# Two-layer attention and perception kernel: spread key loads, five split half groups, shared value buffers, late pointwise weights

## The chip, the cores and the metric

The kernel runs on one core of a Trainium2 chip. The metric is the device time of one launch in microseconds; lower is better. Engines are named as in the profile: PE (matmul), PEld (weight load), DVE (VectorE), ACT (ScalarE), POOL (GpSimd) and SP (SyncE, which here only issues transfers).

## The reference

Input `x` is (4, 64, 64, 256) in float32. Two layers follow each other.

```python
# layer 0: full self-attention over the 4096 pixels of an image
q, k, v = x @ Wq + bq, x @ Wk + bk, x @ Wv + bv      # widths 32, 32, 256
attn = softmax(einsum('bnd,bmd->bnm', q, k))
h = gamma * (attn @ v) + x
# layer 1: depthwise 3x3 (3 outputs a channel), two pointwise layers, 3x3 local attention
perceived = depthwise_conv3x3(h, w_perc) + b_perc    # 256 -> 768 channels
hid = gelu(w_up1 @ perceived + b_up1)                # 768 -> 512
h_new = h + w_up2 @ hid + b_up2                      # 512 -> 256
out = h_new + local_attention3x3(h_new)              # softmax over 9 neighbours
```

## The kernel before

**Slots and points.** The 4 images are cut into 8 blocks of 512 pixels each, so there are 32 *slots* (`NSLOT`), one per block of queries, eight to an image. A slot runs over the image's 8 key blocks (*groups*, `G`), each in two halves of 256 keys, so it has 16 *points*. One software pipeline, written out by hand in the loop over slots and points, interleaves both layers. In each point the program emits, in this order: loads of keys and values for two groups ahead (`load_keys`, `load_values`), the energies and exponentials two points ahead (`energy`), the load of value forms three points ahead (`load_forms`), the jobs of layer 1 for older slots (`jobs[point]`), the weighted sum `product` of this point, the denominators of the next point (`add_up`), and a number of depthwise steps taken from `share[point]`. Each engine takes its instructions in this order. The depthwise conv (`perceive`) of a slot has 60 DVE steps: three rounds of 16 tap steps (L585) and 4 mixing steps (L591).

**Parts.** Most half groups are a plain fp32 product: 8 matmul instructions of `p` with `v` (L398). The half groups in `IN_PARTS` are done in parts: `p` and `v` are split into a high part, a remainder and a "gap" form, and 12 fp32r matmuls replace the 8 (L410). This costs ACT one more pass (`ph`, L384) and DVE two more (`pl` L429, `pg` L430), emitted in `add_up` one point before the product. The value forms are made once in `project_v` and kept in DRAM (`packed_f`). Slots 0 and 31 have no parts.

**End of a slot.** `partial_sums` turns the denominators (DVE, L453 and L454), a small matmul `dps` (PE, L472) adds them over partitions, and `finish` scales the four accumulator banks into the ring `xp`; the next slot's energies and jobs come behind `dps` on PE. The job `local_values` in point 10 leaves a PSUM bank that DVE must empty (`lv`, L887).

**Boundaries.** In slots 7, 15 and 23 the projections of the next image are done as well, after every second point (`nxt`): `project_v` twice and, for even blocks, `project_qk`, whose result `st` goes to DRAM (`packed`). Slot 0 does the same for the rest of the first image. Keys come back from `packed` with each row needed twice: `load_parts` uses two transfers of 64 rows, the outer dimension of the transfer being the 2.

**Buffers.** One ring of four buffers `late` holds `ph`, `pl`, `pg` and the loaded forms `vf`; `vs` (three) holds what `project_v` writes out; `st` is its own. Two buffers hold keys (`ka`), three hold values (`v`). PSUM has two `m` banks for all jobs and `dps`, four `acc` banks and one two-bank tile for energies.

Of the kernel before, what the change touches and what calls it, by code (L numbers as in the profile page):

```python
# [16 lines left out]
P = 128  # L17
# [33 lines left out]
BELOW = 1.0 - 2.0**-13  # L51
IN_PARTS = (2, 6, 10, 14)

# [5 lines left out]
def attention_then_perception_kernel(  # L59
# [37 lines left out]
    def unshifted():  # L97
# [113 lines left out]
        packed_f = tc.dram_tile([P, NSLOT * 2, 3, 2 * C], F32, name="packed_f")  # L211

        def in_parts(s, G, half):
            return 0 < s < NSLOT - 1 and 2 * G + half in IN_PARTS
# [37 lines left out]
        def project_qk(s):  # L252

            ps = bank("m", f"qk_{s}")
            for kin in range(CH):
                for r in range(2):
                    nc.tensor.matmul(
                        ps[2 * r * CQK : 2 * (r + 1) * CQK, :],
                        lhsT=wqk[:, kin].rearrange("p s d -> p (s d)"),
                        rhs=staged[s + r][:, kin, :], start=(kin == 0), stop=(kin == CH - 1),  # L260
                    )
            if s == 2:
                both = tile_of([P, TPB, C], "late", "st_2", 4).rearrange(
                    "p (a t) c -> p a (t c)", a=2
                )
            else:
                both = tile_of([P, 2, NB], "st", f"st_{s}")
            high, low = both[:, 0, :], both[:, 1, :]
            nc.scalar.activation(high.bitcast(F32R), ps, AF.Identity, bias=bqk2)
            nc.scalar.activation(low, ps, AF.Identity, bias=bqk2)  # L270
            nc.vector.tensor_tensor(low, low, high, ALU.subtract)
            if s == 0:
                queries[0] = tile_of([P, NB], "qa", "qa_0", 2)
                for G in range(2):
                    keys[0, G] = tile_of([P, NB], "ka", f"ka_0_{G}", 2)
                for part, G in ((0, 0), (1, 0), (0, 1), (1, 1)):
                    for i in range(2):
                        for to, at, from_ in (
                            (queries[0], 2 * i + part, 0), (keys[0, G], 2 * part + i, 2 * G + 1)
                        )[G:]:  # L280
                            rows, of = (slice(j * CQK, (j + 1) * CQK) for j in (at, from_))
                            nc.sync.dma_start(out=to[rows, :], in_=both[of, part, :])
            nc.sync.dma_start(
                out=packed[s // 2].rearrange("a r q d n -> (r q d) a n"), in_=both
            )

# [21 lines left out]
        def load_forms(s, G, half):  # L308
            forms[s, G, half] = tile_of([P, TPB, C], "late", f"vf_{s}_{G}_{half}", 4)
            nc.sync.dma_start(  # L310
                out=forms[s, G, half].rearrange("p (f t) c -> p f (t c)", f=2),
                in_=packed_f[:, 2 * block(s, G) + half, 1:3],
            )

        def fresh(name):
            return tile_of([P, 2, C], "vs", name, 3)

        def project_v(s, pair, tag="m"):
# [11 lines left out]
            if not split or s < NBLK or s >= NSLOT - NBLK:  # L330
                if s >= NBLK:
                    v = fresh(f"vs_{s}_{pair}")
                else:
                    if pair == 0:
                        values[0, s] = tile_of([P, TPB, C], "v", f"v_0_{s}", 3)
                    v = values[0, s][:, 2 * pair : 2 * pair + 2, :]
                nc.scalar.activation(v, of, AF.Identity, scale=SPLIT / (SPLIT + 1.0))
                nc.scalar.dma_start(
                    out=packed_v[:, bass.ts(2 * s + pair, 2 * C)],
                    in_=v.rearrange("p t c -> p (t c)"),  # L340
                )
            if split:
                whole, high, low = (fresh(f"v{n}_{s}_{pair}") for n in "whl")
                nc.scalar.copy(whole, of)
                nc.scalar.activation(high.bitcast(F32R), of, AF.Identity, scale=BELOW)
                nc.vector.tensor_tensor(low, whole, high, ALU.subtract)
                gap = fresh(f"vg_{s}_{pair}")
# [23 lines left out]
        def energy(s, G, half):  # L371
# [9 lines left out]
            weights[s, G, half] = p  # L381
            if in_parts(s, G, half):
                high = tile_of([P, 2, NB], "late", f"ph_{s}_{G}_{half}", 4)
                nc.scalar.activation(high.bitcast(F32R), p, AF.Identity, scale=BELOW)  # L384
                highs[s, G, half] = high

        def product(s, G, half):
            p = weights[s, G, half]
            first = G == 0 and half == 0
            if first:  # L390
                n = 2 * CH if 0 < s < NSLOT - 1 else CH
                accs[s] = [bank("acc", f"acc_{s}_{c}") for c in range(n)]
# [24 lines left out]
        def add_up(s, G, half):  # L417
# [8 lines left out]
            if in_parts(s, G, half):  # L426
                high = highs[s, G, half]
                low, gap = (tile_of([P, 2, NB], "late", f"p{n}_{s}_{G}_{half}", 4) for n in "lg")
                nc.vector.tensor_tensor(low.bitcast(F32R), p, high, ALU.subtract)  # L429
                nc.vector.scalar_tensor_tensor(  # L430
                    gap.bitcast(F32R), low, -SPLIT, high, ALU.mult, ALU.add
                )
                lows[s, G, half], gaps[s, G, half] = low, gap
# [32 lines left out]
        def finish(s, parts=((0, RB),)):  # L466
# [16 lines left out]
            for r0, r1 in parts:  # L483
                n = slice(r0 * W, r1 * W)
                for c, o in enumerate(os):
                    total = acc[c]
                    if 0 < s < NSLOT - 1:
                        nc.vector.tensor_tensor(o, acc[c], o, ALU.add)
                        total = o
                    nc.vector.scalar_tensor_tensor(  # L490
                        o[:, n], total[:, n], gam[:, 0:1], rden[:, n], ALU.mult, ALU.mult,
                        accum_out=seen(),
# [51 lines left out]
        def spare(s, name):  # L544
            tag = "v" if s == NSLOT - 1 else "late"
            return tile_of([P, TPB, C], tag, name, 3 if tag == "v" else 4).rearrange(
                "p (a t) c -> p a (t c)", a=2
            )

# [72 lines left out]

        wmix = pool.tile([P, 4, MULT, C], F32, tag="wmix", name="wmix")

        def mix_weights(y11, y12, y21, y22, t1, t2, t3, t4):
            for to, a, b in ((t1, y12, y11), (t2, y22, t1), (t3, y22, y12), (t4, y21, t2)):
                nc.gpsimd.tensor_tensor(to, a, b, ALU.subtract)
# [8 lines left out]
        def hidden_part(s, d, part):  # L638
# [8 lines left out]
            y22 = lambda j: wup1[:, MULT + j, bass.ts(d + 2, P)]  # L647
            t1, t2, t3, t4 = (lambda j, i=i: wmix[:, i, j, bass.ts(d, P)] for i in range(4))

# [343 lines left out]
        def local_reciprocal(s):  # L993
            inverse = tile_of([P, 2, NJ], "inverse", f"linverse_{s}")[:, 0, :]
            turned = tile_of([P, NB], "st", f"lturned_{s}")
            nc.vector.transpose(turned, totals.pop(s))
# [62 lines left out]
        nc.vector.tensor_scalar(gbv, gbv, gam[:, 0:1], None, ALU.mult)  # L1059
        nc.vector.tensor_scalar(gam, gam, 1.0 + 1.0 / SPLIT, None, ALU.mult)  # L1060
        wlv = pool.tile([P, CH, C], F32, tag="wlv", name="wlv")
# [10 lines left out]
        for slot in range(NSLOT):  # L1072
# [27 lines left out]

            share = [4, 4, 5, 6, 5, 3, 6, 4, 4, 4, 4, 4, 3, 2, 2, 0]
            if slot == NSLOT - 1:
# [21 lines left out]
            for point in range(points):  # L1124
                G, half = divmod(point, 2)
                after = slot + (G + 1) // NG, (G + 1) % NG
                if half == 0:
# [12 lines left out]
                for do in jobs[point]:  # L1140
                    do()
                product(slot, G, half)

# [17 lines left out]
                if slot == 0 and point == NG:  # L1161
# [8 lines left out]
                    mix_weights(  # L1170
                        *blocks_of(wup1, MULT, C), *(wmix[:, i] for i in range(4))
                    )
# [478 lines left out]
```

## Time and profile before

| | |
|---|---|
| median of 3 runs | 3391.0 us (3388.3 to 3391.58) |
| the profiled execution | 3390.54 us, of which the span of the program is 3388.7 us |
| PE busy | 3329.8 us (98% of the span) |
| DVE busy | 2833.7 us (84%) |
| ACT, POOL busy | 1256.2 us (37%), 413.1 us (12%) |
| mean granted TensorE clock | 0.993 |
| data moved by DMA | 358.51 MB, 106 GB/s over the span |

A row of a windows view gives a stretch of the span, then for each engine its busy time and number of instructions, then the granted clock (1.00 is full), the share of the 16 DMA engines' time in use and the rate. A timeline row gives start, length, engine, line, operation, tile written and tiles read, and how many instructions are merged in it; in brackets stands the idle time of the engine before it and who ended it. Instructions of one engine overlap a little in these rows, so costs below are taken from one start to the next.

### The profile page before, as it was taken

To read this page: it belongs to the slowest core of one execution; us is meant where nothing else is said; L and a number is where in the kernel's file an instruction comes from. 1 tells how busy PE (TensorE), PEld (TensorE's weight loads), DVE (VectorE), ACT (ScalarE), POOL (GpSimd) and SP (SyncE) were. 2 spreads that over 40 slices of the span, in tenths; PEclk is the share of its full clock that TensorE was granted. 3 is DMA by queue.
4 is the path that set the end of the run, shared out by engine and by line. 5 is a ranking of instruction groups with operands and counts; after the bars stand their busy time and mean duration, and the time that the engine had idled before them with its cause. 6 is when DMAs were issued, how large, how long until landed. Compare 5 with 4: busy or idle time off the path is not lost.

```text
span 3388.7 us, 33590 instructions
## 1 busy us (share of the span) xinstructions
PE 3329.8 (98%) x11654; PEld 2115.8 (62%) x11654; DVE 2833.7 (84%) x4188; ACT 1256.2 (37%) x1548; POOL 413.1 (12%) x590
## 2 busy tenths in 40 slices
PE   9989999999999999999999999999899999999998
PEld 5546666666666666666666666666566666666655
DVE  2488898877889998986898899887588999999995
ACT  3333434333433333333333433333333343333331
POOL 2100011101111100111011111101100111111031
PEclk9989999999999999999999999999999999999999
DMA  5432232353233323345333333324522333332100
GB/s 175 158 112 96 93 103 97 112 168 120 96 105 101 110 86 104 99 126 171 102 98 100 99 102 103 104 94 141 166 86 98 98 98 102 104 108 90 63 16 27
DMA packets 203109, 358.51 MB, mean 106 GB/s; under 512 B 71748, under 2 KB 72404, under 8 KB 202804
## 3 DMA queue, kind: packets, MB, share of 16 engines
q1 hardware_dynamic: 189972, 326.16, 30.6%
q0 software_dynamic: 4416, 15.11, 1.3%
q10 hardware_dynamic: 8544, 15.01, 1.2%
q8 instruction: 95, 1.56, 0.2%
q14 instruction: 82, 0.67, 0.1%
HBM read 303.01 MB, written 52.43 MB: 105 GB/s over the span
## 4 chain that ended last, share of the span: by engine, by line
PE 88%; issue 4%; DMA 3%; DVE 3%; ACT 1%; SPq 1%; POOL 0%; ACTq 0%; DVEq 0%; POOLq 0%
PE acc L398 37%; PE acc L410 9%; PE e L375 7%; PE dx L711 6%; PE hid_gf L654 4%; PE hid_de L654 4%; PE hid_bc L654 4%; PE lv L874 3%; PE g L807 3%; PE lo L1008 3%; PE s L915 2%; PE hid_a L654 2%; PE v L323 2%; DMA ka<-packed 2%; DVE perc L585 1%
## 5 line engine op out<-in xcount | busy, mean ns | idle before, releaser
L398 PE MATMUL acc<-p,v 128*128 128x512 f32 x3136 | 1421.2, 596 | 0.0
L585 DVE SCALAR_TENSOR_TENSOR perc<-xp,wperc,perc 128x526 f32<-128x526 f32 (+3 forms) x1554 | 1115.8, 778 | 31.1 <-ACT perc L581 31.0
L380 ACT ACTIVATE p<-e 128x1024 f32<-128x1024 f32 x512 | 523.9, 1023 | 1395.6 <-PE e L375 1215.7
L398 PEld LDWEIGHTS acc<-p,v 128*128 128x128 f32 x3136 | 593.8, 191 | 624.8 <-issue 610.9
L425 DVE TENSOR_TENSOR den<-den,p 128x1024 f32<-128x1024 f32 x480 | 593.5, 1236 | 45.4 <-ACT p L380 43.3
L375 PE MATMUL e<-qa,ka 128*128 128x512 f32 x1024 | 457.5, 528 | 30.2 <-DMA ka<-packed 17.3
L940 POOL TENSOR_TENSOR lp<-lp,near 128x396 f32<-128x396 f32 x60 | 86.6, 1443 | 2160.8 <-ACT lp L935 2160.8
L375 PEld LDWEIGHTS e<-qa,ka 128*128 128x128 f32 x1024 | 190.1, 190 | 214.6 <-issue 178.7
L711 PE MATMUL dx<-hid,wup 128*128 128x512 f32 x512 | 229.8, 592 | 0.0
L963 POOL TENSOR_TENSOR lsum<-lsum,lp 128x99 f32<-128x99 f32 (+1 forms) x179 | 176.0, 990 | 11.7
L654 PE MATMUL hid_de<-perc,wmix 128*128 128x256 f32 x720 | 165.0, 378 | 0.0
L591 DVE TENSOR_TENSOR perc<-perc 128x262 f32<-128x262 f32 x360 | 156.7, 449 | 6.3
L677 ACT ACTIVATE hid<-hid,bup 128x512 f32<-128x512 f32 x120 | 80.1, 715 | 216.5 <-DVE hid L661 216.5
L430 DVE SCALAR_TENSOR_TENSOR pg<-pl,ph 128x1024 fp32r<-128x1024 f32 x120 | 154.9, 1291 | 4.1
L711 PEld LDWEIGHTS dx<-hid,wup 128*128 128x128 f32 x512 | 96.9, 189 | 98.0 <-issue 92.8
L410 PE MATMUL acc<-ph,v 128*128 128x512 f32 x480 | 155.3, 445 | 0.0
L429 DVE TENSOR_TENSOR pl<-p,ph 128x1024 fp32r<-128x1024 f32 x120 | 150.5, 1254 | 0.0
L654 PEld LDWEIGHTS hid_de<-perc,wmix 128*128 128x128 f32 x720 | 135.9, 189 | 21.0
L581 ACT ACTIVATE perc<-xp,bperc,wperc 128x526 f32<-128x526 f32 (+1 forms) x192 | 147.2, 815 | 1.7 <-DVE xp L496 1.7
L410 PE MATMUL acc<-pl,vf 128*128 128x512 f32 x480 | 130.3, 393 | 4.4 <-DVE pl L429 4.4
L410 PE MATMUL acc<-pg,vf 128*128 128x512 f32 x480 | 129.6, 392 | 0.1
L384 ACT ACTIVATE ph<-p 128x1024 fp32r<-128x1024 f32 x120 | 127.0, 1058 | 3.8
(183 smaller groups left out, 3583.2 us busy)
## 6 DMA issues: line engine op xcount, KB each, us to landing
v<-packed_v SPq DMA_DIRECT2D x128, 512.0 KB
ka<-packed SPq DMA_DIRECT2D x508, 128.0 KB
vf<-packed_f SPq DMA_DIRECT2D x120, 512.0 KB
v<-packed_f SPq DMA_DIRECT2D x120, 256.0 KB
v<-packed_v SPq DMA_DIRECT2D x120, 256.0 KB
xp<-in_x SPq DMA_DIRECT2D x30, 528.0 KB
xc<-in_x SPq DMA_DIRECT2D x56, 256.0 KB
out<-lo SPq DMA_DIRECT2D x56, 256.0 KB
```

Of the source, the lines that this page charges most:

```text
L375: nc.tensor.matmul(e[:, i, :], lhsT=keys[s, G][:, bass.ts(2 * half + i, P)].bitcast(F32R), rhs=queries[s].bitcast(F32R), start=True, stop= ...
L380: nc.scalar.activation(p, e, AF.Exp)
L398: nc.tensor.matmul(accs[s][c], lhsT=v[:, i, bass.ts(c, P)], rhs=p[:, i, :], start=(first and i == 0), stop=(last and i == 1),)
L410: nc.tensor.matmul(accs[s][to + c], lhsT=w[:, i, bass.ts(c, P)].bitcast(F32R), rhs=x[:, i, :].bitcast(F32R), start=(to > 0 and n == 0 and ...
L425: nc.vector.tensor_tensor(den, den, p, ALU.add)
L429: nc.vector.tensor_tensor(low.bitcast(F32R), p, high, ALU.subtract)
L430: nc.vector.scalar_tensor_tensor(gap.bitcast(F32R), low, -SPLIT, high, ALU.mult, ALU.add)
L585: nc.vector.scalar_tensor_tensor(acc, win, wt, acc, ALU.mult, ALU.add)
L591: nc.vector.tensor_tensor(t[:, to, :], t[:, a, :], t[:, b, :], op)
L654: nc.tensor.matmul(ps[:, n * C : (n + 1) * C], lhsT=w(j), rhs=rows_of(mixes[s, j][:, kind, :]), start=(j == 0), stop=(j == MULT - 1),)
L711: nc.tensor.matmul(ps, lhsT=wup2[:, d, bass.ts(c, P)], rhs=hids[s][:, d, :], start=(d == 0), stop=(d == NHC - 1),)
L963: nc.gpsimd.tensor_tensor(to, to, near_ws[block, half][:, t_, of, :], ALU.add)
```

## The change

- `load_parts` issues four transfers of 32 rows where it issued two of 64, for keys and queries.
- `IN_PARTS` is (2, 5, 8, 11, 14) where it was (2, 6, 10, 14), so five half groups a slot are in parts; slot 2 (`LAG_PERC`) joins slots 0 and 31 in having none.
- The four `late` buffers go. `ph`, `pl`, `pg` have one buffer each, `vf` two. `ph` is made one point later, ahead of that point's exponential (`high_part`).
- `vs` has four buffers and also takes `st` (as two tiles, stored by two transfers) and a transposed tile; in the first image `st` uses `o`, in slot 2's pair `pg`. The copy `whole` of a split is dropped (`low` takes it), and the plain pair of a block is projected before the split pair.
- `w_up1` and `w_up2` are loaded in slot 1 where they were loaded in slot 0; one of the four mixed weight blocks is kept in place of a block of `wup1`, which is loaded again in the last slot.
- `share` is a new list, with the same sum of 60. The scaled gamma gets its own tile.

```diff
-IN_PARTS = (2, 6, 10, 14)
+IN_PARTS = (2, 5, 8, 11, 14)
+        def in_two_sums(s):
+            return 0 < s < NSLOT - 1 and s != LAG_PERC
         def load_parts(to, s, which):
             pair, r = divmod(s, 2)
-            part = packed[pair, :, r, which]
-            for i in range(2):
-                of = part[i : i + 1].to_broadcast([2, CQK, NB]) if which else part
-                nc.sync.dma_start(out=to[2 * i * CQK : 2 * (i + 1) * CQK, :], in_=of)
+            for i in range(4):
+                of = packed[pair, i // 2 if which else i % 2, r, which]
+                nc.sync.dma_start(out=to[i * CQK : (i + 1) * CQK, :], in_=of)
...
-                both = tile_of([P, 2, NB], "st", f"st_{s}")
-            high, low = both[:, 0, :], both[:, 1, :]
+                tag, bufs = ("o", 2) if s < NBLK else ("vs", 4)
+                parts = high, low = [tile_of([P, NB], tag, f"st_{s}_{i}", bufs) for i in range(2)]
...
-            nc.sync.dma_start(
-                out=packed[s // 2].rearrange("a r q d n -> (r q d) a n"), in_=both
-            )
+            for i, part in enumerate(parts):
+                nc.sync.dma_start(
+                    out=packed[s // 2, i].rearrange("r q d n -> (r q d) n"), in_=part
+                )
...
-            forms[s, G, half] = tile_of([P, TPB, C], "late", f"vf_{s}_{G}_{half}", 4)
+            forms[s, G, half] = tile_of([P, TPB, C], "vf", f"vf_{s}_{G}_{half}", 2)
...
-                whole, high, low = (fresh(f"v{n}_{s}_{pair}") for n in "whl")
-                nc.scalar.copy(whole, of)
+                low, high = (fresh(f"v{n}_{s}_{pair}") for n in "lh")
+                nc.scalar.copy(low, of)
...
-            return [lambda: project_v(s, 0), lambda: project_v(s, 1)] + pair
+            order = sorted(range(2), key=lambda n: 2 * (s % NBLK) + n in IN_PARTS)
+            return [lambda n=n: project_v(s, n) for n in order] + pair
...
+        def high_part(s, G, half):
+            high = tile_of([P, 2, NB], "ph", f"ph_{s}_{G}_{half}")
+            nc.scalar.activation(high.bitcast(F32R), weights[s, G, half], AF.Identity, scale=BELOW)
+            highs[s, G, half] = high
...
-        wmix = pool.tile([P, 4, MULT, C], F32, tag="wmix", name="wmix")
+        wmix = pool.tile([P, 3, MULT, C], F32, tag="wmix", name="wmix")
...
-            share = [4, 4, 5, 6, 5, 3, 6, 4, 4, 4, 4, 4, 3, 2, 2, 0]
+            share = [1, 3, 7, 7, 1, 3, 7, 3, 5, 6, 2, 5, 6, 1, 3, 0]
...
+                behind = slot + (point + 1) // points, *divmod((point + 1) % points, 2)
+                if in_parts(*behind):
+                    high_part(*behind)
                 if after[0] < NSLOT:
                     energy(*after, half)
...
+                if slot == NSLOT - 1 and point == NHC + 2 * RING:
+                    nc.sync.dma_start(out=wup1[:, :MULT, C:], in_=w_up1[:, :MULT, C:])
...
+                if slot == 1 and point == 2:
                     wup1 = loaded(w_up1, "wup1", queue=nc.gpsimd)
                     bup1 = loaded(b_up1, "bup1", queue=nc.gpsimd)
+                if slot == 1 and point == NG:
                     wup2 = loaded(w_up2, "wup2", queue=nc.gpsimd)
```

More of the change, by code (lines that the diff above doesn't have):

```diff
@@ L211, in unshifted @@
         packed_f = tc.dram_tile([P, NSLOT * 2, 3, 2 * C], F32, name="packed_f")
+        def in_two_sums(s):
+            return 0 < s < NSLOT - 1 and s != LAG_PERC
         def in_parts(s, G, half):
-            return 0 < s < NSLOT - 1 and 2 * G + half in IN_PARTS
+            return in_two_sums(s) and 2 * G + half in IN_PARTS
         def load_parts(to, s, which):
             pair, r = divmod(s, 2)
-            part = packed[pair, :, r, which]
-            for i in range(2):
-                of = part[i : i + 1].to_broadcast([2, CQK, NB]) if which else part
-                nc.sync.dma_start(out=to[2 * i * CQK : 2 * (i + 1) * CQK, :], in_=of)
+            for i in range(4):
+                of = packed[pair, i // 2 if which else i % 2, r, which]
+                nc.sync.dma_start(out=to[i * CQK : (i + 1) * CQK, :], in_=of)
         def fetch(s):
@@ L262, in project_qk @@
             if s == 2:
-                both = tile_of([P, TPB, C], "late", "st_2", 4).rearrange(
-                    "p (a t) c -> p a (t c)", a=2
-                )
-            else:
-                both = tile_of([P, 2, NB], "st", f"st_{s}")
-            high, low = both[:, 0, :], both[:, 1, :]
+                both = tile_of([P, 2, NB], "pg", "st_2")
+                parts = high, low = both[:, 0, :], both[:, 1, :]
+            else:
+                tag, bufs = ("o", 2) if s < NBLK else ("vs", 4)
+                parts = high, low = [tile_of([P, NB], tag, f"st_{s}_{i}", bufs) for i in range(2)]
             nc.scalar.activation(high.bitcast(F32R), ps, AF.Identity, bias=bqk2)
@@ L281, in project_qk @@
                             rows, of = (slice(j * CQK, (j + 1) * CQK) for j in (at, from_))
-                            nc.sync.dma_start(out=to[rows, :], in_=both[of, part, :])
-            nc.sync.dma_start(
-                out=packed[s // 2].rearrange("a r q d n -> (r q d) a n"), in_=both
-            )
+                            nc.sync.dma_start(out=to[rows, :], in_=parts[part][of, :])
+            for i, part in enumerate(parts):
+                nc.sync.dma_start(
+                    out=packed[s // 2, i].rearrange("r q d n -> (r q d) n"), in_=part
+                )
         def block(s, G):
@@ L315, in fresh @@
         def fresh(name):
-            return tile_of([P, 2, C], "vs", name, 3)
+            return tile_of([P, NB], "vs", name, 4).rearrange("p (t c) -> p t c", c=C)
         def project_v(s, pair, tag="m"):
@@ L333, in project_v @@
                 else:
-                    if pair == 0:
+                    if (0, s) not in values:
                         values[0, s] = tile_of([P, TPB, C], "v", f"v_0_{s}", 3)
@@ L342, in project_v @@
             if split:
-                whole, high, low = (fresh(f"v{n}_{s}_{pair}") for n in "whl")
-                nc.scalar.copy(whole, of)
+                low, high = (fresh(f"v{n}_{s}_{pair}") for n in "lh")
+                nc.scalar.copy(low, of)
                 nc.scalar.activation(high.bitcast(F32R), of, AF.Identity, scale=BELOW)
-                nc.vector.tensor_tensor(low, whole, high, ALU.subtract)
+                nc.vector.tensor_tensor(low, low, high, ALU.subtract)
                 gap = fresh(f"vg_{s}_{pair}")
@@ L381, in energy @@
             weights[s, G, half] = p
[L382 to L385, printed above, removed]
+        def high_part(s, G, half):
+            high = tile_of([P, 2, NB], "ph", f"ph_{s}_{G}_{half}")
+            nc.scalar.activation(high.bitcast(F32R), weights[s, G, half], AF.Identity, scale=BELOW)
+            highs[s, G, half] = high
         def product(s, G, half):
@@ L390, in product @@
             if first:
-                n = 2 * CH if 0 < s < NSLOT - 1 else CH
+                n = 2 * CH if in_two_sums(s) else CH
                 accs[s] = [bank("acc", f"acc_{s}_{c}") for c in range(n)]
@@ L427, in add_up @@
                 high = highs[s, G, half]
-                low, gap = (tile_of([P, 2, NB], "late", f"p{n}_{s}_{G}_{half}", 4) for n in "lg")
+                low, gap = (tile_of([P, 2, NB], f"p{n}", f"p{n}_{s}_{G}_{half}") for n in "lg")
                 nc.vector.tensor_tensor(low.bitcast(F32R), p, high, ALU.subtract)
@@ L486, in finish @@
                     total = acc[c]
-                    if 0 < s < NSLOT - 1:
+                    if in_two_sums(s):
                         nc.vector.tensor_tensor(o, acc[c], o, ALU.add)
@@ L490, in finish @@
                     nc.vector.scalar_tensor_tensor(
-                        o[:, n], total[:, n], gam[:, 0:1], rden[:, n], ALU.mult, ALU.mult,
+                        o[:, n], total[:, n], gam_parts[:, 0:1], rden[:, n], ALU.mult, ALU.mult,
                         accum_out=seen(),
@@ L544, in spare @@
         def spare(s, name):
[L545 to L548, printed above, removed]
+            if s == NSLOT - 1:
+                return tile_of([P, TPB, C], "v", name, 3).rearrange("p (a t) c -> p a (t c)", a=2)
+            spares.append(spares.pop(0))
+            return tile_of([P, 2, NB], spares[-1], name)
+        spares = ["ph", "pl", "pg"]
         def perceive(s, steps):
@@ L620, in unshifted, with mix_weights @@
         lower = by_turns(range(NPC), range(LOW, TAPS), RB - 1, RB)
-        wmix = pool.tile([P, 4, MULT, C], F32, tag="wmix", name="wmix")
-        def mix_weights(y11, y12, y21, y22, t1, t2, t3, t4):
-            for to, a, b in ((t1, y12, y11), (t2, y22, t1), (t3, y22, y12), (t4, y21, t2)):
+        wmix = pool.tile([P, 3, MULT, C], F32, tag="wmix", name="wmix")
+        def mix_weights(y11, y12, y21, y22, t1, t2, t4):
+            for to, a, b in ((t1, y12, y11), (t2, y22, t1), (t4, y21, t2), (y12, y22, y12)):
                 nc.gpsimd.tensor_tensor(to, a, b, ALU.subtract)
@@ L647, in hidden_part @@
             y22 = lambda j: wup1[:, MULT + j, bass.ts(d + 2, P)]
-            t1, t2, t3, t4 = (lambda j, i=i: wmix[:, i, j, bass.ts(d, P)] for i in range(4))
+            t1, t2, t4 = (lambda j, i=i: wmix[:, i, j, bass.ts(d, P)] for i in range(3))
+            t3 = lambda j: wup1[:, j, bass.ts(d + 2, P)]
             def products(name, *todo):
@@ L994, in local_reciprocal @@
             inverse = tile_of([P, 2, NJ], "inverse", f"linverse_{s}")[:, 0, :]
-            turned = tile_of([P, NB], "st", f"lturned_{s}")
+            turned = tile_of([P, NB], "vs", f"lturned_{s}", 4)
             nc.vector.transpose(turned, totals.pop(s))
@@ L1059, in unshifted @@
         nc.vector.tensor_scalar(gbv, gbv, gam[:, 0:1], None, ALU.mult)
-        nc.vector.tensor_scalar(gam, gam, 1.0 + 1.0 / SPLIT, None, ALU.mult)
+        gam_parts = pool.tile([P, 1], F32, tag="gam_parts", name="gam_parts")
+        nc.vector.tensor_scalar(gam_parts, gam, 1.0 + 1.0 / SPLIT, None, ALU.mult)
         wlv = pool.tile([P, CH, C], F32, tag="wlv", name="wlv")
@@ L1166, in unshifted @@
                     bperc = loaded(b_perc, "bperc", queue=nc.gpsimd)
+                if slot == 1 and point == 2:
                     wup1 = loaded(w_up1, "wup1", queue=nc.gpsimd)
                     bup1 = loaded(b_up1, "bup1", queue=nc.gpsimd)
+                if slot == 1 and point == NG:
                     wup2 = loaded(w_up2, "wup2", queue=nc.gpsimd)
                     mix_weights(
-                        *blocks_of(wup1, MULT, C), *(wmix[:, i] for i in range(4))
+                        *blocks_of(wup1, MULT, C), *(wmix[:, i] for i in range(3))
                     )
```

## The prediction

> **What bounds the kernel now.** I read the page's busy times first, then a windows view cut at the slots, then PE's waits, then the timelines of one steady slot.
>
> ```profile
> PE 3329.8 (98%) x11654; PEld 2115.8 (62%) x11654; DVE 2833.7 (84%) x4188; ACT 1256.2 (37%) x1548; POOL 413.1 (12%) x590
> ```
>
> ```profile
> 24.80:122.50 97.70, 89.83 (x267) 49.11 (x267) 28.94 (x35) 28.70 (x38) 18.51 (x24) 0.95 0.52 162
> 122.50:194.10 71.60, 66.78 (x208) 37.84 (x206) 38.45 (x44) 24.38 (x26) 0.62 (x2) 0.95 0.41 128
> 194.10:270.10 76.00, 69.35 (x201) 39.03 (x198) 72.82 (x105) 26.18 (x30) 0.61 (x2) 0.93 0.36 114
> 1817.20:1915.10 97.90, 97.90 (x345) 62.75 (x344) 88.98 (x133) 37.51 (x45) 11.85 (x14) 1.00 0.31 100
> 655.10:795.80 140.70, 135.06 (x505) 88.36 (x504) 97.85 (x145) 53.09 (x73) 15.04 (x26) 1.00 0.54 160
> 2306.40:2461.00 154.60, 141.56 (x505) 91.10 (x504) 97.85 (x145) 55.48 (x77) 15.68 (x26) 0.96 0.50 153
> ```
>
> Rows 1 to 3 are slots 0 to 2, row 4 the steady slot 18, the last two the boundary slots 7 and 23 (slot 15 has 140.9 us). A steady slot is PE without a gap; DVE is busy 89 of its 97.9 us. PE idles only at the start and at the boundaries, where the clock also falls below 1.00. So the gain must come from less PE work in steady slots, or from those gaps, and DVE has 9 us a slot to give.
>
> ```profile
> PE e L375 <- DMA ka<-packed: 17.3, 8, 4.8
> PE acc L410 <- DVE pl L429: 4.4, 2, 3.9
> ```
>
> Late keys are the longest of PE's waits. The end of the steady slot, on DVE from the `lv` of point 10 and on PE:
>
> ```profile
> 1884.36 0.76 DVE L887 TENSOR_TENSOR lv<-lv,blv 128x256 f32<-128x256 f32 x2 [1.47 <-PE lv L874]
> ...
> 1898.41 1.40 DVE L429 TENSOR_TENSOR pl<-p,ph 128x1024 fp32r<-128x1024 f32 x1
> 1899.85 1.48 DVE L430 SCALAR_TENSOR_TENSOR pg<-pl,ph 128x1024 fp32r<-128x1024 f32 x1
> ...
> 1907.59 0.69 DVE L454 TENSOR_REDUCE parts<-turned 128x16 f32<-128x512 f32 x1
> 1909.16 0.36 DVE L475 RECIPROCAL inverse<-dps 128x32 f32<-128x32 f32 x1 [0.88 <-PE dps L472]
> ```
>
> ```profile
> 1903.08 1.09 PE L410 MATMUL acc<-pl,vf 128*128 128x512 f32 x4
> ...
> 1908.82 0.30 PE L472 MATMUL dps<-parts,fold 128*128 128x32 f32 x2
> ```
>
> From 1884.36 to 1908.28 DVE never idles: 23.92 us. PE wants the sums at 1908.82, 0.54 us later. In the other steady slots this margin is 0.4 to 0.5 us (once less). DVE's spare time lies ahead of point 10; at the slot's end there is none. This is what decides.
>
> **Steady slots, PE.** In slot 1, where no jobs stand between:
>
> ```profile
> 179.26 3.60 PE L398 MATMUL acc<-p,v 128*128 128x512 f32 x8
> 182.30 1.03 PE L375 MATMUL e<-qa,ka 128*128 128x512 f32 x2
> 183.16 1.07 PE L410 MATMUL acc<-ph,v 128*128 128x512 f32 x4
> 184.07 1.07 PE L410 MATMUL acc<-pl,vf 128*128 128x512 f32 x4
> 184.98 1.07 PE L410 MATMUL acc<-pg,vf 128*128 128x512 f32 x4
> 185.88 0.62 PE L375 MATMUL e<-qa,ka 128*128 128x512 f32 x2
> ```
>
> A plain half group with the energies behind it takes 3.90 us (179.26 to 183.16), one in parts 3.18 (183.16 to the next plain product at 186.34): 0.7 us saved. 29 slots of 5 against 30 of 4 are 145 against 120: 25 x 0.7 = 17 us less PE work in all, 0.7 a steady slot.
>
> **Steady slots, DVE.** A further `pl` and `pg` cost 1.25 + 1.15 = 2.40 us from start to start where POOL is quiet. Over the slot they fit. Over its end they do not: before, points 10 to 15 hold one pair (for 14) and 15 steps of `share` (4+4+3+2+2+0); after, two pairs (for 11 and 14) and 17 steps (2+5+6+1+3+0). The steps come in rounds of 16 taps and 4 mixes; the four mixes of the third round lie in this stretch both times, so it gains two taps of 0.68. The stretch becomes 23.92 + 2.40 + 1.36 = 27.68 us. It starts 0.7 us sooner, since by point 10 three of five half groups are already in parts instead of two; the DVE idle ahead of `lv` (1.47 here, 1.97 in most slots) pays for the two steps more in points 7 to 9 and is then about 0.5. So the sums end 3.76 - 0.70 = 3.06 us later than now, PE has 0.45 us of margin, and the slot grows by 2.6 us to 100.5. PE shows it as two waits: about 1.7 us before `pl` at point 14 (`pl` would end near 1904.0 on this slot's clock; PE comes for it at 1903.08 - 0.70 = 1902.4) and the rest before `dps`. Where the slot's block has an edge row (6 of the 24), 0.8 us more border work in point 7 finds 0.5 us less idle: 0.35 each.
>
> That holds in slots 4 to 6, 8 to 14, 16 to 22 and 24 to 30: 24 x 2.6 + 6 x 0.35 = **+64 us**. Slot 3 has no local sums yet and stays.
>
> The uncertain part is POOL. Clean DVE work in the stretch adds up to 21.2 us; 2.7 us are delays while POOL multiplies masks and sums windows (L940, L963): a tap that meets L940 takes 1.38 instead of 0.68, `pl` and `pg` 0.2 more each, one `den` 0.5. After the change taps meet L963, which no steady slot shows. Bounds: 1.3 us less (only the L940 delays stay), +1.3 a slot, 31 us; 0.7 us more, +3.3, 80 us. I keep the sum of 2.7, since POOL's instructions are the same and DVE is never idle there in either.
>
> `ph` ahead of the exponential costs nothing: ACT idles 2 to 6 us ahead of most exponentials and `p` is a point old. Four key loads cost SP about 1 us more a group (0.5 an issue); a group lasts 10 us and more in a steady slot.
>
> **Start.** Adding up the points' excess over the same point without a gap, slot 0 loses 13.1 us, slot 1 8, slot 2 12.2, idle and half clock together. The key waits come from the transfer's shape: in the trace's semaphore records a key load issued at 236.05 us gets its last two engines' counts at 246.16, 10 us later, while a 32-row `ka<-st` issued at 11.43 has all sixteen by 13.40. The nearest row for the new loads is that one: 2 us, and 1 us more of issue. The Trainium skill ("DMA: Bandwidth & Descriptors", "Why a DMA increments its semaphore by 16 and not by 1") says that the number of engines divides the slowest dimension, so 2 for the old shape and 16 for the new; no run here shows it yet for a load from DRAM.
>
> Slot 0: late keys (7.4 us with the slow clock) leave about 2, since the first exponentials wait for `gbv`; the stop of ACT behind the weights' transfers (5.7 us) goes: -11. Slot 1: -8 of key stalls, -0.7, and +2 for the weights' 2 MB now beside its loads (0 if hidden, 6 if it stops SP as in slot 0, where one key issue took 7.6 us): -7. Slot 2: without parts 15 x 3.89 + 8.0 = 66.4 instead of 76.0, and DVE's 65 us fit: -9.5. Together **-27** (-16 to -33).
>
> **Boundaries.** 97.8 + 16 x 1.73 (`project_v`) + 4 x 1.87 (`project_qk`) = 133; the slots take 7, 7 and 21 us more. Spread keys remove the key waits and ACT's waits for stores queued on the two loaded engines. What is late next: `st` now shares `vs` with the forms. In block 4 ACT must wait with `st`'s low part until POOL's store of `low` has landed (DVE 1.8 us, issue 0.5, 2.7 to 4.4 to land), and queued behind it are `ph` and the exponential of points 11 and 12, and on DVE the subtraction of `st` with everything after: 2 us on PE, then some 2 at `dps`; and the split of block 7 now ends after the denominators, ahead of the reciprocal that frees an `m` bank: 1 to 1.5. I leave 5 us in each: -3, -3, -16 = **-22** (-12 to -37).
>
> **Sum.** 3390.5 + 64 - 27 - 22 = 3405.5; the profiled execution lies 0.5 us under the median, which I neglect.
>
> A rule against this change stands in "TensorE: Matmul & The Clock Gate" (The HAM clock gate): the clock halves after an idle window of 3.4 us. By it the new waits cost no clock. The trace is stricter: after 1.96 us idle up to 2423.33 the clock was 0.51 for 3.4 us, while 2.07 us up to 1612.18 cost none. Waits of 1.7 stay under both, so I add nothing.
>
> **Rivals.** (1) POOL's delays shrink because taps and POOL's short sums interleave better: below +2.05 us a slot (49 us over 24 slots) the change is a gain. For: nothing shows the new pairing. Against: a constant 2.7 us in 24 slots. At +1.3: 3390.5 + 33 - 49 = 3374. (2) The DVE end costs what I say, but start and boundaries give back all they lose (33 + 37): 3385. For: their causes are mostly DMA. Against: `st` behind the stores. (3) The loads do not spread, so the change doesn't do what it says: only slot 2 and ACT's stop gain some 15 us: 3440.
>
> **How the numbers follow.** Forecast 0.48, (1) 0.24, (2) 0.20, (3) 0.08. About 0.2% (7 us) is what a measurement of this kernel can tell from no change. Forecast and (3) give slower by more, except a sixth of the forecast: 0.48; (1) and half of (2) faster: 0.34; the rest 0.18. The forecast's own range is 3390 to 3436 (mainly 24 x 0.7 up, and 10 us of start and boundaries down). The whole range goes down to 3352, which is POOL's lower bound with the largest gains at start and boundaries (3390.5 + 31 - 33 - 37), and up to 3436.
>
> **What would show it.** Right: slots 0 to 2 near 87, 65 and 66 us; steady slots near 100.5 with PE waiting for `pl` and for `parts`; key waits gone. Wrong: steady slots at 97.2 without gaps, `lv` to sums under 25 us, or key loads whose last counts still come 10 us late.

## The result, and the profile after

The changed kernel takes 3414.8 us (median of 4 runs, 3413.4 to 3416.0) against 3389.7 us for the kernel before on the same chip: ratio 1.0074, 95% interval 1.0057 to 1.0092. It is slower by 25 us; 3405 was forecast. The profiled execution has a span of 3412.8 us, 24.1 us more than before.

The page's busy times and its row for the key loads (line, engine, operation, count, KB each, median us to landing):

```profile
PE 3330.4 (98%) x11754; PEld 2131.2 (62%) x11754; DVE 2901.1 (85%) x4248; ACT 1277.1 (37%) x1577; POOL 457.4 (13%) x602
ka<-packed SPq DMA_DIRECT2D x1016, 64.0 KB, 1.9
```

PE's busy time did not fall by the 17 us of work that five parts save, since part of each wait counts as busy: slot 21 takes 3.3 us more than the same five parts without waits (97.38 us, below), and the view has PE idle for 2.56 of them. Half clock counts as busy too, but the mean clock hardly moved (0.993 before, 0.994 after). The windows view by slots (columns as before; the rows are slots 0, 1, 2, then the steady slots 18 and 21, then the boundary slots 7 and 23):

```profile
25.00:110.90 85.90, 85.09 (x267) 47.27 (x266) 30.59 (x38) 29.60 (x40) 9.04 (x18) 1.00 0.56 166
110.90:179.40 68.50, 65.22 (x213) 38.57 (x211) 46.90 (x46) 24.46 (x26) 14.73 (x12) 0.98 0.54 170
179.40:245.80 66.40, 66.40 (x183) 33.98 (x182) 63.26 (x96) 21.65 (x24) 0.62 (x2) 1.00 0.38 108
1820.10:1921.40 101.30, 99.40 (x350) 64.31 (x349) 91.16 (x135) 38.16 (x46) 11.27 (x14) 0.98 0.33 102
2123.90:2224.60 100.70, 98.14 (x350) 63.25 (x349) 90.42 (x131) 38.20 (x46) 13.02 (x14) 1.00 0.33 102
642.20:777.30 135.10, 133.99 (x510) 89.20 (x509) 101.35 (x148) 54.56 (x75) 18.96 (x29) 1.00 0.59 176
2325.40:2461.50 136.10, 133.96 (x509) 89.05 (x508) 100.70 (x146) 57.56 (x80) 18.96 (x29) 1.00 0.61 184
```

Slot 0 lost 11.8 us, slot 1 3.1, slot 2 9.5, the three boundaries 5.6, 6.1 and 18.5. The steady slots grew: 100.7 us where there were 97.8. PE's waits (total us, times, longest) show on what:

```profile
PE acc L414 <- DVE pl L433: 39.6, 25, 2.0
PE dps L476 <- DVE parts L458: 14.9, 15, 1.1
PE e L378 <- ACT p L383: 5.4, 3, 3.2
```

The waits for keys (17.3 us before) are gone, and in their place stand the two that the prediction named. The timeline of the end of slot 21:

```profile
2190.49 0.75 DVE L894 TENSOR_TENSOR lv<-lv,blv 128x256 f32<-128x256 f32 x2 [0.32 <-PE lv L881]
...
2202.41 5.52 DVE L591 SCALAR_TENSOR_TENSOR perc<-xp,wperc,perc 128x526 f32<-128x526 f32 x6
2207.85 1.61 DVE L429 TENSOR_TENSOR den<-den,p 128x1024 f32<-128x1024 f32 x1
2209.38 1.39 DVE L433 TENSOR_TENSOR pl<-p,ph 128x1024 fp32r<-128x1024 f32 x1
2210.82 1.21 PE L414 MATMUL acc<-pl,vf 128*128 128x512 f32 x4 [1.49 <-DVE pl L433]
...
2217.45 0.69 DVE L458 TENSOR_REDUCE parts<-turned 128x16 f32<-128x512 f32 x1
2218.20 0.41 PE L476 MATMUL dps<-parts,fold 128*128 128x32 f32 x2 [0.94 <-DVE parts L458]
```

From `lv` to the end of the sums DVE takes 27.65 us without idling (27.68 was worked out). Six taps stand right ahead of the `den` and `pl` of point 14; PE waits 1.49 us for that `pl` and another 0.94 us for the sums, which come 0.06 us before PE starts `dps`.

Summed by groups of slots, from the first product of a slot to that of the next: the 24 steady slots +75.5 us, slot 3 +1.6, slots 0 to 2 -24.4, the boundaries -30.2, all together +22.5. Of the 1.6 us to the span's 24.1, 1.4 lie in the last 50 us of the program, where the profile's clock is 0.90 after and 0.94 before.

### The profile page after: what moved, and what is told of

It is laid out like the page before. It is cut to its first block, busy times and chain, and to the rows that moved or that the text cites. A ratio compares the mean times of both kernels' runs of the same rounds, so it can differ in the third digit from the quotient of the medians.

```text
span 3412.8 us, 34590 instructions
## 1 busy us (share of the span) xinstructions
PE 3330.4 (98%) x11754; PEld 2131.2 (62%) x11754; DVE 2901.1 (85%) x4248; ACT 1277.1 (37%) x1577; POOL 457.4 (13%) x602
## 4 chain that ended last, share of the span: by engine, by line
PE 74%; DVE 23%; issue 1%; ACT 1%; SPq 0%; DMA 0%; ACTq 0%; DVEq 0%; POOL 0%; POOLq 0%
PE acc L402 26%; DVE perc L591 10%; PE acc L414 8%; PE dx L718 6%; DVE den L429 5%; PE e L378 5%; PE hid_bc L661 5%; PE hid_gf L661 5%; PE hid_de L661 5%; PE v L325 3%; PE lv L881 3%; PE lo L1015 3%; PE g L814 2%; DVE pl L433 2%; PE hid_a L661 2%; DVE pg L434 2%
## 5 line engine op out<-in xcount | busy, mean ns | idle before, releaser
L402 PE MATMUL acc<-p,v 128*128 128x512 f32 x2936 | 1323.8, 594 | 0.2 <-ACT v L339 0.2
L402 PEld LDWEIGHTS acc<-p,v 128*128 128x128 f32 x2936 | 556.2, 191 | 586.7 <-issue 570.4
L414 PE MATMUL acc<-pl,vf 128*128 128x512 f32 x580 | 162.1, 402 | 39.6 <-DVE pl L433 39.6
L414 PE MATMUL acc<-ph,v 128*128 128x512 f32 x580 | 185.0, 441 | 0.0
L434 DVE SCALAR_TENSOR_TENSOR pg<-pl,ph 128x1024 fp32r<-128x1024 f32 x145 | 177.6, 1225 | 7.4
L433 DVE TENSOR_TENSOR pl<-p,ph 128x1024 fp32r<-128x1024 f32 x145 | 182.2, 1257 | 0.0
L414 PE MATMUL acc<-pg,vf 128*128 128x512 f32 x580 | 167.5, 412 | 3.1 <-DVE pg L434 0.3
L414 PEld LDWEIGHTS acc<-pl,vf 128*128 128x128 f32 x580 | 108.2, 190 | 74.0 <-DVE pl L433 51.2
L388 ACT ACTIVATE ph<-p 128x1024 fp32r<-128x1024 f32 x145 | 152.3, 1050 | 0.2
L414 PEld LDWEIGHTS acc<-pg,vf 128*128 128x128 f32 x580 | 110.3, 194 | 38.5 <-DVE pg L434 14.7
```

What stands on the lines that cost most here:

```text
L388: nc.scalar.activation(high.bitcast(F32R), weights[s, G, half], AF.Identity, scale=BELOW)
L402: nc.tensor.matmul(accs[s][c], lhsT=v[:, i, bass.ts(c, P)], rhs=p[:, i, :], start=(first and i == 0), stop=(last and i == 1),)
L414: nc.tensor.matmul(accs[s][to + c], lhsT=w[:, i, bass.ts(c, P)].bitcast(F32R), rhs=x[:, i, :].bitcast(F32R), start=(to > 0 and n == 0 and ...
L434: nc.vector.scalar_tensor_tensor(gap.bitcast(F32R), low, -SPLIT, high, ALU.mult, ALU.add)
```

## The experiments

All results in one table. Ratios are to the kernel before, run on the same chip. The last four columns are slot times in us from the profiled execution of each: the mean of the 24 steady slots, the sum of slots 0 to 2, slot 3, and the sum of the three boundary slots.

| kernel | median us | ratio, 95% | steady | 0 to 2 | 3 | 7+15+23 |
|---|---|---|---|---|---|---|
| before | 3389.7 | 1 | 97.70 | 245.2 | 94.8 | 436.2 |
| after | 3414.8 | 1.0074 (1.0057 to 1.0092) | 100.84 | 220.8 | 96.4 | 406.0 |
| after, old step list | 3376.4 | 0.9962 (0.9948 to 0.9976) | 99.32 | 218.6 | 94.3 | 406.9 |
| after, four parts, old list | 3338.9 | 0.9851 (0.9835 to 0.9868) | 97.89 | 217.4 | 94.9 | 407.5 |
| before, four key loads | 3366.4 | 0.9928 (0.9911 to 0.9944) | 97.69 | 223.9 | 94.8 | 436.3 |
| after, two key loads | 3451.7 | 1.0182 (1.0165 to 1.0199) | 100.83 | 238.5 | 96.4 | 425.3 |
| after, front-loaded list | 3329.9 | 0.9831 (0.9814 to 0.9847) | 97.38 | 220.7 | 94.3 | 407.3 |
| after, quiet POOL | 3345.7 | 0.9879 (0.9863 to 0.9896) | 98.12 | 220.9 | 94.9 | 405.9 |
| before, four key loads, new pair order | 3357.2 | 0.9913 (0.9896 to 0.9929) | 97.70 | 224.3 | 94.8 | 424.0 |
| after, early weights | 3409.6 | 1.0068 (1.0051 to 1.0085) | 100.88 | 216.7 | 96.4 | 406.0 |
| front-loaded list, early weights | 3325.8 | 0.9818 (0.9804 to 0.9831) | 97.35 | 215.9 | 94.3 | 407.2 |
| the same, six parts | 3307.9 | 0.9765 (0.9752 to 0.9779) | 96.76 | 215.9 | 94.4 | 403.6 |
| after, three `vs` buffers | 3423.2 | 1.0107 (1.0092 to 1.0123) | 100.87 | 219.3 | 96.4 | 415.3 |
| early weights, seven parts | 3369.7 | 0.9950 (0.9934 to 0.9967) | 98.91 | 220.8 | 95.4 | 406.7 |

### The end of the steady slot

**The old step list in the changed kernel.**

```diff
-            share = [1, 3, 7, 7, 1, 3, 7, 3, 5, 6, 2, 5, 6, 1, 3, 0]
+            share = [4, 4, 5, 6, 5, 3, 6, 4, 4, 4, 4, 4, 3, 2, 2, 0]
```

> The changed kernel with the step list of before (15 steps in points 10 to 15 where the new list has 17). Theory: DVE's stretch from lv to the sums sets the steady slot; two taps of 0.68 us less make it 27.7 - 1.36 = 26.3 us, so a steady slot falls from 100.7 to 99.3 us and the kernel from 3415 to about 3382 us (24 x 1.36 = 33 us). Rival A, POOL's delays set the length and the number of taps does not: steady slots stay at 100.7 us, 3415 us. Rival B, the new list is needed to fit five pairs into the middle of the slot: PE gets new waits before point 10 and the time is above 3415 us.

3376.4 us; the stretch from `lv` to the sums is 26.33 us in slot 21 and the slot 99.38. PE's long waits for `pl` are gone, the wait for the sums is left (two rows of the timeline, then PE's wait):

```profile
2162.78 0.75 DVE L894 TENSOR_TENSOR lv<-lv,blv 128x256 f32<-128x256 f32 x2 [1.67 <-PE lv L881]
...
2188.42 0.69 DVE L458 TENSOR_REDUCE parts<-turned 128x16 f32<-128x512 f32 x1
```

```profile
PE dps L476 <- DVE parts L458: 25.5, 22, 1.2
```

With the same five pairs, two taps moved ahead of `lv` are worth 38 us (1.53 us a steady slot, 1.36 expected), and the change is faster than the kernel before. Rivals A and B fall.

**Four parts.**

```diff
-IN_PARTS = (2, 5, 8, 11, 14)
+IN_PARTS = (2, 6, 10, 14)
```

with the old list again.

> The changed kernel with four half groups in parts (2, 6, 10, 14) and the step list of before; loads, buffers, order of the pairs and place of the weights stay as changed. Theory: the loss is all in the fifth pair and the steps at the slot's end, 24 x 3.15 = 75.6 us and 1.6 us in slot 3, less 0.7 us in slot 1: steady slots 97.8 us without gaps, 3415 - 76.5 = about 3338 us, below the kernel before by some 52 us. Rival: the single buffers of ph, pl and pg, or the exponential behind ph, cost something in steady slots by themselves: steady slots above 98.5 us, 3355 us or more.

3338.9 us, steady slots 97.89 us: within 1 us of the sum. So the fifth pair and the step list are the whole loss, and all the rest of the change (the buffers, `ph` a point later, the spread loads) costs a steady slot about 0.2 us.

**Without POOL's work at the slot's end.**

```diff
-                nc.gpsimd.tensor_tensor(pv, pv, mask, ALU.mult)
+                pass
...
-            nc.gpsimd.memset(t, 0.0)
-            for half in range(2):
-                for (block, t_), rows, of in pieces(s):
-                    to = tv[:, rows, columns(half)]
-                    nc.gpsimd.tensor_tensor(to, to, near_ws[block, half][:, t_, of, :], ALU.add)
+            nc.gpsimd.memset(t, 1.0)
```

> The changed kernel without POOL's multiplication by the neighbour mask and without its sums over windows (a constant stands in their place), so layer 1 leaves out the mask and its denominators. Theory: 2.7 us of DVE's 27.7 us from lv to the sums are delays beside POOL; without them the stretch is about 25 us, the steady slot 98.0 us, and the kernel 3415 - 24 x 2.7 = about 3350 us. Rival: the pairs and steps fill the 27.7 us by themselves and POOL costs little: stretch above 27 us, 3400 us or more.

3345.7 us; the stretch is 25.00 us and slot 21 takes 98.04 us (the windows view: POOL is busy 2.69 us of it, 13.0 in the changed kernel). The ends of the stretch in the timeline, then the slot in the windows view:

```profile
2147.88 0.76 DVE L894 TENSOR_TENSOR lv<-lv,blv 128x256 f32<-128x256 f32 x2 [0.32 <-PE lv L881]
...
2172.19 0.69 DVE L458 TENSOR_REDUCE parts<-turned 128x16 f32<-128x512 f32 x1
```

```profile
2081.30:2179.34 98.04, 97.59 (x349) 63.41 (x348) 87.73 (x131) 38.07 (x46) 2.69 (x8) 1.00 0.33 105
```

POOL delays DVE by 2.65 us in this stretch (27.65 - 25.00), as much as the 2.7 us that were worked out for the kernel before; the first rival of the prediction, that these delays shrink, is out.

**A list with less at the end.**

```diff
-            share = [1, 3, 7, 7, 1, 3, 7, 3, 5, 6, 2, 5, 6, 1, 3, 0]
+            share = [5, 4, 6, 6, 5, 4, 6, 4, 4, 4, 3, 3, 3, 1, 2, 0]
```

> The changed kernel with a third step list: 48 steps in points 0 to 9 and 12 in points 10 to 15 (the changed kernel has 43 and 17, the kernel before 45 and 15): [5, 4, 6, 6, 5, 4, 6, 4, 4, 4, 3, 3, 3, 1, 2, 0]. Theory: with three taps less at the end than with the list of before, the sums come 3 x 0.68 = 2.0 us sooner, less 0.4 us because lv then starts later; PE's last waits (1.2 us for the sums, 0.7 us at point 14) go, and the steady slot falls to 97.3 to 97.6 us, below the 98.0 us of four parts: 3376 - 24 x 2 = about 3328 us. Rival: the steps moved ahead delay the evictions of the hidden jobs, PE waits for a bank of m before point 10, and the steady slot stays at 98.5 us or more: 3352 us or more.

3329.9 us. Slot 21, in the windows view:

```profile
2069.28:2166.66 97.38, 97.38 (x350) 63.42 (x348) 90.37 (x131) 38.19 (x46) 12.89 (x14) 1.00 0.33 106
```

PE has no gap again and does five parts in 97.38 us; DVE is busy 90.37 us, just as in the changed kernel (90.42 of 100.7). Not DVE's amount of work cost 75 us but where in the slot it stands. `lv` did not come 0.4 us later, as I had it: DVE still idles 1.68 us ahead of it, as with the old list (1.67). The three steps moved forward fill DVE's other idle stretches ahead of it, which in slot 21 shrink from 5.7 to 3.8 us. The sums now come only 0.06 to 0.11 us before PE starts `dps`, so five parts with this list have no margin left at the slot's end.

### Start and boundaries

**Four key loads alone, in the kernel before.**

```diff
-            part = packed[pair, :, r, which]
-            for i in range(2):
-                of = part[i : i + 1].to_broadcast([2, CQK, NB]) if which else part
-                nc.sync.dma_start(out=to[2 * i * CQK : 2 * (i + 1) * CQK, :], in_=of)
+            for i in range(4):
+                of = packed[pair, i // 2 if which else i % 2, r, which]
+                nc.sync.dma_start(out=to[i * CQK : (i + 1) * CQK, :], in_=of)
```

> The kernel before with nothing changed but load_parts, which issues four transfers of 32 rows. Theory: the key waits (17.3 us) and the half clock and exponential waits that hang on them go: about -30 us, 3360 us, with slots 7, 15 and 23 near 137 us and steady slots at 97.8 us. Rival: the gain at start and boundaries came from the order of the pairs, st in two tiles and the late weights: -10 us or less, 3380 us or more.

3366.4 us: between the two. In the profiled execution all of the gain comes from slots 0 to 2 (-21.3 us) and the boundaries gain nothing; that execution is the slowest of four (3370.8 us), and where the two at 3363 us gain their 7 us was not seen. PE no longer waits for keys there, but one thing later. ACT in slot 7, from the timeline:

```profile
767.76 0.60 ACT L336 ACTIVATE vs<-v 128x512 f32<-128x512 f32 x1 [6.28 <-DMA packed_f<-vh]
```

ACT idles 6.28 us until the store of a form frees one of the three `vs` buffers, and PE behind it waits 3.1 us in that slot.

**Two key loads in the changed kernel**, the same edit backwards.

> The changed kernel with two transfers of 64 rows for keys and queries, as before. Theory: start and boundaries lose again what the loads gave, about 30 us: 3445 us, with counts of the key loads that come 9 us and more after the issue, and slots 7, 15 and 23 near 140 us and more. Rival: with the rest of the change the keys come early enough either way: 3420 us or less. Both expect steady slots near 100.7 us, since keys are loaded a group ahead there.

3451.7 us, 37 us more; the boundaries take 425.3 us and PE's waits have the keys back:

```profile
PE e L379 <- DMA ka<-packed: 27.1, 12, 4.5
```

**The projection part, with four key loads, in the kernel before.**

```diff
...
-                whole, high, low = (fresh(f"v{n}_{s}_{pair}") for n in "whl")
-                nc.scalar.copy(whole, of)
+                low, high = (fresh(f"v{n}_{s}_{pair}") for n in "lh")
+                nc.scalar.copy(low, of)
...
-                nc.vector.tensor_tensor(low, whole, high, ALU.subtract)
+                nc.vector.tensor_tensor(low, low, high, ALU.subtract)
...
-            return [lambda: project_v(s, 0), lambda: project_v(s, 1)] + pair
+            order = sorted(range(2), key=lambda n: 2 * (s % NBLK) + n in IN_PARTS)
+            return [lambda n=n: project_v(s, n) for n in order] + pair
```

> The kernel before with four key loads of 32 rows (3366 us alone) and in addition the projection part of the change: the plain pair of a block ahead of the split pair, and no separate tile for the whole value, so a split takes three vs buffers instead of four. Theory: the boundaries' waits for vs buffers and for the reciprocal come from the split that holds all three buffers until its stores land; slots 7, 15 and 23 fall from 142, 143 and 151 us to about 136 each, 3366 - 28 = 3338 us. Rival: it is st in tiles of vs and its two stores, or the fourth vs buffer, that matter: boundaries stay above 139 us, 3355 us or more.

3357.2 us: the rival. Slot 23 gains 10.6 us, slots 7 and 15 stay at 141.9 and 141.3.

**Three `vs` buffers in the changed kernel.**

```diff
-                tag, bufs = ("o", 2) if s < NBLK else ("vs", 4)
+                tag, bufs = ("o", 2) if s < NBLK else ("vs", 3)
...
-            return tile_of([P, NB], "vs", name, 4).rearrange("p (t c) -> p t c", c=C)
+            return tile_of([P, NB], "vs", name, 3).rearrange("p (t c) -> p t c", c=C)
...
-            turned = tile_of([P, NB], "vs", f"lturned_{s}", 4)
+            turned = tile_of([P, NB], "vs", f"lturned_{s}", 3)
```

> The changed kernel with three vs buffers instead of four, st still in two of them. Theory: the fourth buffer is what frees the boundaries, since four 32-row loads with the new order of the pairs still left them at 424 us in sum: slots 7, 15 and 23 go from 406 to 420 us or more, 3429 us. Rival: with st in tiles that go as soon as they are stored, three are enough: 3418 us or less.

3423.2 us, and 415.3 us at the boundaries: half way between the two theories. The fourth buffer is worth 9 us, 7 of them in slot 23. So the boundary's 30 us come in steps: nothing for the loads alone (436.3 us), 12 with the pair order and without `whole` (424.0), 9 with the rest of the change but three buffers (415.3), 9 with the fourth buffer (406.0). The loads are needed all the same: taken back alone at the end, they lose 19 us. Which part of "the rest" gives the third step (`st` in tiles of its own that go as they are stored is the likely one) was not tried alone.

**Early weights in the changed kernel**: both conditions `slot == 1` back to `slot == 0 and point == NG`.

> The changed kernel with the pointwise weights loaded and mixed in slot 0, as before. Theory: slot 0 gets back the stop of ACT behind the weights' transfers, +5 us (about 91 us), and slot 1 loses the 3 us in which DVE's three den and pl took 2.8 us each beside POOL's four mixes (about 65 us): +2 us in sum, 3417 us. Rival: the weights cost the same 5 us in either slot: 3415 us. Rival: slot 1 has no other use for the room and stays at 68 us: 3420 us.

3409.6 us: slot 1 takes 63.4 us (65 were expected), 5.1 less than with the late weights, and slot 0 only 86.9, 1.0 more (91 were expected). With spread loads the stop of ACT behind the weights is nearly gone by itself: the kernel before with four key loads, whose weights are early too, takes 85.9 us in slot 0. In slot 1 the late weights cost this (DVE and POOL, from the timelines):

```profile
120.78 8.44 DVE L429 TENSOR_TENSOR den<-den,p 128x1024 f32<-128x1024 f32 x3
129.14 2.82 DVE L433 TENSOR_TENSOR pl<-p,ph 128x1024 fp32r<-128x1024 f32 x1
```

```profile
119.67 2.92 POOL L635 TENSOR_TENSOR wmix<-wup 128x768 f32<-128x768 f32 x1 [7.47 <-DMA wup<-in_w_up]
122.67 5.47 POOL L635 TENSOR_TENSOR wmix<-wup,wmix 128x768 f32<-128x768 f32 x2
128.09 2.79 POOL L635 TENSOR_TENSOR wup<-wup 128x768 f32<-128x768 f32 x1
```

While POOL makes its four mixes (the last is `wup<-wup`), each `den` and `pl` of DVE takes 2.8 us instead of 1.14 and 1.25, and each mix 2.7 to 2.9 where it takes 1.8 with DVE idle (in the kernel before with four key loads): the two engines take turns. PE then waits 3.2 us for an exponential, and the next 3.4 us run at half clock. The Trainium skill ("Trainium Architecture — The Big Picture", "What this means for kernel authors") says that these two engines share one pair of memory ports and that the share is an exclusive lock, not a split of bandwidth. The five rows agree: one DVE operation for each POOL operation. The meeting alone is not what costs slot 1 its time, though. With the early weights it happens in slot 0:

```profile
85.26 8.40 DVE L429 TENSOR_TENSOR den<-den,p 128x1024 f32<-128x1024 f32 x3
```

PE waits for nothing there. In slot 1 the last of the delayed operations is a `pl`, which slot 0, without parts, does not have: ACT idles 7.33 us before the next exponential until that `pl` has ended, and PE waits behind ACT.

### Versions that beat both

**The front-loaded list with early weights.**

> The changed kernel with the front-loaded step list (3330 us) and the pointwise weights loaded in slot 0 again. Theory: the two parts add up, since one acts in steady slots and the other in slots 0 and 1: slot 1 at 63.4 us, 3330 - 4 = 3326 us. Rival: the 4 to 5 us of the early weights were a chance of that run's transfers: 3330 us.

3325.8 us: the two add up.

**Six parts**, on top of that, with the further pair ahead of `lv`.

```diff
-IN_PARTS = (2, 5, 8, 11, 14)
+IN_PARTS = (2, 4, 6, 8, 11, 14)
-            share = [5, 4, 6, 6, 5, 4, 6, 4, 4, 4, 3, 3, 3, 1, 2, 0]
+            share = [5, 5, 7, 4, 6, 3, 6, 4, 5, 3, 3, 3, 3, 1, 2, 0]
```

> As the front-loaded list with early weights, but six half groups in parts (2, 4, 6, 8, 11, 14), the further pair ahead of lv, and 48 steps in points 0 to 9: [5, 5, 7, 4, 6, 3, 6, 4, 5, 3, 3, 3, 3, 1, 2, 0]. Theory: what counts is DVE's work behind lv and not its sum; DVE idles some 4.5 us ahead of lv and 2.4 us of it take the pair, so PE's saving of 0.7 us a slot is kept: steady slots 96.7 us, 3326 - 17 + 3 for the further split at each boundary = about 3312 us. Rival: DVE with 92.8 us in a slot is full, evictions ahead of lv come late and PE waits: steady slots 97.4 us or more, 3326 us or more.

3307.9 us, 2.3% below the kernel before. Slot 21:

```profile
2053.43:2150.17 96.74, 96.74 (x354) 64.16 (x353) 92.51 (x133) 39.49 (x47) 12.90 (x14) 1.00 0.35 112
```

The boundaries got faster by 3.6 us instead of slower by 3. DVE's idle time ahead of `lv` is down to 0.57 us, and 0 in slots with an edge row, which take 97.1 us.

**Seven parts.**

```diff
-IN_PARTS = (2, 4, 6, 8, 11, 14)
+IN_PARTS = (2, 4, 6, 8, 10, 12, 14)
-            share = [5, 5, 7, 4, 6, 3, 6, 4, 5, 3, 3, 3, 3, 1, 2, 0]
+            share = [5, 5, 7, 4, 6, 3, 6, 4, 6, 2, 4, 2, 3, 1, 2, 0]
```

> As the version with six half groups in parts (3308 us), but seven (2, 4, 6, 8, 10, 12, 14), with 48 steps in points 0 to 9: [5, 5, 7, 4, 6, 3, 6, 4, 6, 2, 4, 2, 3, 1, 2, 0]. Theory: DVE has 0.57 us of idle time left ahead of lv and none behind; a further pair of 2.4 us comes 1.8 us late there, PE saves 0.7 us, so the steady slot is about 96.8 - 0.7 + 1.8 = 97.9 us and the kernel 3308 + 24 x 1.1 = about 3335 us, with PE's waits for pl or for the sums back. Rival: evictions can come later still without holding PE: steady slots at 96.1 us, 3292 us.

3369.7 us, 62 us more than with six parts where 27 were expected. Slot 21 takes 98.67 us, with PE's waits for `pl` (1.1 us) and for the sums (0.6) back. The timelines show why it is 1.9 us more than with six parts and not 1.1. `lv` starts 67.75 us into the slot instead of 65.95, the 1.8 us as worked out, and the stretch behind it is 24.46 us instead of 24.32, so the sums come 1.9 us later and the slot ends 1.9 us later. The expectation took PE's 0.7 us off that, but PE's saving cannot shorten a slot whose end DVE sets. Slot 0 took 6.3 us longer than with the front-loaded list and early weights (92.27 against 85.95): ACT idles 5.4 us there until the store of a form has freed a `vs` buffer, PE waits 4.1 us for the exponential behind it, and 6.8 us at half clock follow.

## Why the prediction was right, and where its sum was off

**Steady slots: right in mechanism, place and length of the stretch.** 27.68 us were worked out, 27.65 measured; 1.7 us of wait before `pl` and the rest before `dps`, 1.5 and 0.9 measured. The term was too small by 11.5 us (64 against 75.5). In an undisturbed slot it is 2.9 us instead of 2.6: `lv` comes 0.59 us sooner, not 0.70, PE starts `dps` 0.06 us after the sums, and the slot's end behind `dps` takes 0.1 us more. Edge slots grew by 3.5 instead of 2.95. "Waits of 1.7 stay under both, so I add nothing" was wrong: the half clock that I left out is there, nine stretches of 3.4 us in steady slots (the last section says which waits bring it). It costs little, because PE then waits for DVE anyway: slots 5, 12 and 24, which have one, take 101.1 us where their neighbours without one take 100.7.

**Slot 3** was put at no change and grew by 1.6 us. Its sums had 3 us to spare before, but `pl` of point 14 is due ahead of them: PE waits 1.02 us for it, and some more inside the groups of `pl` and `pg`. I checked the margin at one deadline of two.

**Start: -24.4 against -27.** Slot 2 came out as worked (-9.5). Slot 0 did in number (-11.8 against -11), but that is luck: 5.7 us of it were put down to the weights, "the stop of ACT behind the weights' transfers goes". With spread loads the early weights cost 1.0 us, and the loads alone, with early weights, already give the whole 11.8 us (97.7 to 85.9). And in slot 1 I priced the moved transfers (2 us), and not the four `wmix` operations that move with them: -3.1 instead of -7. The move of the weights as a whole loses 4 us where I counted a gain.

**Boundaries: -30 against -22, inside the bounds.** I left 5 us in each slot for what is late next; about 2 are left in slots 7 and 15 and 3 in slot 23 over the 133 us of work. That the loads do it was half of the reason: taken back alone they lose 19 of the 30 us, but given alone they gain nothing there in the profiled execution, since a `vs` buffer is late next. It takes both parts of the change.

**The sum.** 3405 lies within 10 us of 3414.8 partly by luck: the steady slots, slot 3 and the start together came out 16 us higher than worked, the boundaries 8 us lower.

**Rivals.** Smaller POOL delays: excluded by the quiet POOL. Start and boundaries giving back everything: they gave 54.6 of 70 us. Loads that do not spread: 1.9 us to landing. The Trainium skill's rule on the number of engines ("DMA: Bandwidth & Descriptors", "Why a DMA increments its semaphore by 16 and not by 1") now has its row from DRAM: in the semaphore records, four loads issued at 230.21 to 231.49 us have all sixteen counts between 231.93 and 233.54, about 2 us after each issue, where the old form took 10.

## What to carry to other kernels

An engine that is busy 90% of a slot can still set the slot's end: follow its work from the last operation that it must wait for to the next thing that is due, add up that stretch alone, and check every deadline inside it, not only the last. When PE work is traded for DVE work, move DVE's free work ahead of that stretch in the same change: here the same change, with the same five parts, cost 25 us with one list of steps and gained 57 us with another. A transfer that is made faster can move the wait to the next buffer in line, as it did at the boundaries here, and a move of loads moves all that is computed from them on arrival.

## What the runs showed of the hardware that was not expected

**The clock fell to half on a fixed grid of windows, and a window did not have to be idle as a whole.** The beginnings of half clock in one trace lie on one grid of 3.413 us (426.754 and 529.154 us are 30 steps apart). Adding up PE's idle time in each step of that grid, over the traces of all fourteen kernels, without their first and last 30 us: every window at full clock with 1.96 us of idle or more was followed by 3.4 us of half clock or more, none with less than 1.48 us was, and between the two both occur. That fits what puzzled me in the prediction: the 2.07 us of idle up to 1612.18 lay in two windows (1.07 and 1.00), the 1.96 us up to 2423.33 in one. So a single wait of 1.5 us can cost the clock (in the changed kernel one of 1.50 us, alone in its window, did) and another of the same length need not. Waits in one window add up: in the changed kernel with two key loads, one with 2.36 us of idle, in pieces of at most 1.45, was followed by half clock.

**DVE and POOL alternate operation by operation.** In slot 1 of the changed kernel, where POOL's mixes and DVE's `den` and `pl` each read two inputs, operations of the two took turns and none ran at its own pace: 1.14 us became 2.8 on DVE, 1.8 became 2.7 to 2.9 on POOL.
